# A graph layer over 200,000 edges: the window product in three bf16 parts, 29 nodes per half chunk

## The chip, the cores and the metric

One core of a Trainium2 chip runs the whole program in one launch. The metric is the time of one execution on the device, in microseconds (us), and of several executions the median counts. The core has five engines with a queue each: PE (TensorE: products and transposes into PSUM), DVE (VectorE), ACT (ScalarE), POOL (GpSimd) and SP (SyncE, which here only issues DMA transfers). Each runs its instructions in order and meets the others through semaphores.

## The reference

A graph layer on 6250 nodes with 128 features each and 200,000 edges, sorted by destination. Only what is computed by edge matters for what follows:

```python
src = jax.random.randint(..., (200000,), 0, 6250, jnp.int32)
dst = (6250 * jax.random.uniform(..., (200000,)) ** 2.0).astype(jnp.int32)
_o = jnp.argsort(dst, stable=True)
src, dst, edge_attr_4 = src[_o], dst[_o], ...
...
def mesh_conv(x, src, dst, ea, w1, b1, g, bt, w2, b2):
    m = jnp.concatenate([x[dst], x[src], ea], axis=-1) @ w1 + b1
    m = jax.nn.silu(group_norm(m, g, bt))
    m = m @ w2 + b2
    out = jax.ops.segment_sum(m, dst, num_segments=n)
    return out / jnp.clip(cnt, 1.0)[:, None]
...
h = mesh_conv(x, ...)                       # then norm, silu, + time embedding
h = mesh_conv(h, ...)                       # then norm, silu, + x
logits = (q[dst] * k[src]).sum(-1) * scale + (edge_attr @ ew + eb)
w = softmax of logits over the edges of one dst
o = jax.ops.segment_sum(w[:, :, None] * v[src], dst, num_segments=n)
return x_in + h + group_norm(o @ ow + ob, an_g, an_b)
```

All of it is fp32.

## The kernel before, in words

Edges stand in tiles of 128 (one edge a partition), eight tiles make a chunk of 1024 edges, and there are 196 chunks, the last one short (1563 tiles, `EI`). The program has three stages over all chunks: conv 1, conv 2, attention (`pipeline(i, stage)`, line 755). Ahead of them comes the preparation (lines 195 to 333), and each stage ends with `mend` and the last nodes.

*The product of a node with its edges.* The first layer's weights are applied to nodes, not edges: a table `a_d` holds each node's share as a destination, `b_d` (in attention `kv_d`) its share as a source. The source rows are gathered edge by edge, by an indirect DMA from POOL, one a tile (line 661). The destination rows are not gathered: the edges are sorted, so a chunk touches neighbouring nodes. SP loads a window of `WN` = 112 rows of `a_d` from the chunk's lowest node into `pk` (line 647), below it stand the 4 attribute weights and the bias (lines 1056 and 1260). On the other side stands `ohT`: line 631 copies each edge's offset in the window, `rel_d`, onto 112 partitions, for two chunks at a time (`LG`), and line 634 puts the 4 edge attributes and a row of ones below. ACT makes a one-hot of the offsets in two passes, a square of the difference to the partition's number (656, bias `minus_p`) and a Relu (657). One fp32 product of 117 rows a tile then gives the destination's share, the attributes' and the bias at once: `m` in the convolutions (1089), `qe` in attention (1294).

*The rest of a chunk.* In a convolution DVE adds the gathered rows (1096), ACT squares (1098), DVE reduces (1100), normalises (1111 to 1115), ACT takes the silu (1116), DVE builds a one-hot of destinations mod 128 (667), PE sums the edges into their nodes (1121, `u`), and ACT and DVE add that into the table of node sums (1126, 1131). Attention has logits (1309 to 1315), a segmented maximum for up to 8 chunks at a time (1342, 1343), weights (1365) and sums (1372). A function `in_order` (743) fixes the order of the instructions on DVE, SP, ACT and PE as the pipeline wrote them; POOL's gathers run ahead as far as buffers are free (4 in the convolutions, 11 in attention).

*Node batches and side work.* While a stage runs, finished nodes are worked off in batches of 4 windows (`conv_nodes`, 867; `attention_nodes`, 956), 10 batches a stage, at fixed places from about chunk 80 on. They store the next stage's tables. During conv 1 a side task, `deferred` (392), is taken one step a chunk from the fifth chunk on; it loads weights, prepares attention's marks, and counts what the loops below have to do. What is left of it when the first batch is due is run to its end there (lines 790 to 792).

*Edges that don't fit the window.* `relative` (305) sets the offset of every edge that lies `WN` or more beyond the chunk's lowest node to -1 and its `main` to 0; `dm0` (333) is then -1 too, so that the edge takes no part in the fast path. `deferred` finds chunks with such edges (574 to 579, 589 to 591: `trips_i`, the number of 128-node windows of such a chunk), sets `most` to the number of chunks if there is any, and from it `nout_i`, the turns of the loop at 723, and `fix_i` (426 to 440), whether `mend` runs and how many node batches it repeats. `mend` (671) is a run-time loop that is taken once or not at all; in it `leftovers` turns over the chunks, and for each chunk an inner loop (698) over its windows computes the missed edges with loads, gathers and fp32 products of its own, after which the node batches are done again one at a time. The loops of this kind have a meeting of all engines at the end of each turn.

The few lines that matter most:

```python
nc.vector.scalar_tensor_tensor(m, r, float(WN), over(good, c), ALU.is_lt, ALU.mult)        # 308
nc.vector.tensor_scalar(most, most, 0.5, float(NCH), ALU.is_gt, ALU.mult)                   # 593
nc.vector.tensor_scalar(nout_i, most, float(NCH - EI // TPC), 0.0, ALU.subtract, ALU.max)   # 594
with tc.For_i(0, some, 1):                                                                  # 676
with tc.For_i(0, n, 1) as r:                                                                # 698
with tc.For_i(0, nout, 1) as c:                                                             # 723
```

Of the kernel before, what the change touches and what calls it, by code (L numbers as in the profile page):

```python
# [38 lines left out]
KW = WN + KE  # L39
# [10 lines left out]
def kernel(ctx: ExitStack, tc: tile.TileContext, x, src, dst, eat, w, out):  # L50
# [32 lines left out]

    def by_quarter(op, n):

        q = -(-n // 4)
        for a in range(0, n, q):
            op(slice(a, min(a + q, n)))
# [14 lines left out]
    nc.vector.tensor_scalar(minus_p, iota_p, -1.0, None, ALU.mult)  # L103
# [25 lines left out]
    def attribute_rows(pool, i):  # L129
        t = pool.tile([5, D], FP, name="wcb")  # L130
        nc.sync.dma_start(out=t[0:4, :], in_=w[f"c{i}_w1"][2 * D:2 * D + 4, :])
        nc.sync.dma_start(out=t[4:5, :], in_=w[f"c{i}_b1"][None, :])
        return t

# [8 lines left out]
    a_d = {i: dram.tile([(NW + 1) * P, D], FP, name=f"a_d{i}") for i in (1, 2, 3)}  # L143
# [3 lines left out]
    web_d = dram.tile([KE, DB], FP, name="web_d")  # L147
    dwl_d = dram.tile([P, EW], FP, name="dwl_d")
    dmod_d = dram.tile([P, EW], FP, name="dmod_d")
    rel_d = dram.tile([EW, P], FP, name="rel_d")  # L150
# [7 lines left out]
    lo_i = const.tile([P, NCH], I32, name="lo_i")  # L158
# [10 lines left out]
    def by_node(table_d, wi, m):  # L169
        return table_d[wi * P:(wi + m) * P, :].rearrange("(w p) c -> p w c", p=P)  # L170

# [23 lines left out]
    with tc.tile_pool(name="node0", bufs=1) as np_, tc.tile_pool(name="prep", bufs=1) as pp, \  # L195
# [34 lines left out]
        wcb = attribute_rows(rt, 1)  # L230
        centre(rt, wcb, H)
        nc.sync.dma_start(out=wc_d[1], in_=wcb)
# [3 lines left out]
        zeros = np_.tile([P, D], FP, name="zeros")  # L236
# [6 lines left out]
        for a in range(0, NW, 4):  # L243
# [29 lines left out]
        red = pp.tile([P, 2, NCH], FP, name="red")  # L273
        redm = pp.tile([P, 2, NCH], FP, name="redm")
# [3 lines left out]
        nc.vector.tensor_reduce(red[:, 0, :], by_chunk(d_f), AX.X, ALU.min)  # L278
        nc.vector.tensor_scalar(red[:, 0, :], red[:, 0, :], -1.0, None, ALU.mult)
        nc.vector.tensor_tensor(tmp, prev_i, d_i, ALU.is_gt)  # L280
        nc.vector.tensor_scalar(by_chunk(tmp)[:, :, 0], by_chunk(tmp)[:, :, 0], not_first, None, ALU.mult)
        nc.vector.tensor_reduce(red[:, 1, :], by_chunk(tmp), AX.X, ALU.max)
        nc.gpsimd.partition_all_reduce(
            redm.rearrange("p a c -> p (a c)"), red.rearrange("p a c -> p (a c)"), P, bass_isa.ReduceOp.max)


        for a, (m, tT) in keep.items():
# [8 lines left out]
        nc.vector.tensor_scalar(low, redm[:, 0, :], -1.0, None, ALU.mult)  # L296
        good = pp.tile([P, NCH], FP, name="good")
        nc.vector.tensor_scalar(good, redm[:, 1, :], 0.5, None, ALU.is_lt)
        rel = pp.tile([P, EW], FP, name="rel")
        main = pp.tile([P, EW], FP, name="main")  # L300

        def over(t, c):
            return t[:, c, None].to_broadcast([P, c.stop - c.start, TPC])
# [8 lines left out]
        by_quarter(relative, NCH)  # L312
        for k in range(0, EW, 4 * P):
            for _ in to_rows(rel, rel_d, 1.0, pst.tile([P, 4, P], FP, name="tp"),
                             rp.tile([P, 4, P], FP, name="sb"), k, nc.scalar):
                pass

        nc.vector.tensor_copy(lo_i, low)
        nc.vector.tensor_scalar(w0_i, lo_i, 7, None, ALU.arith_shift_right)
        nc.vector.tensor_copy(w0_f, w0_i)  # L320
        lm_i = pp.tile([P, NCH], I32, name="lm_i")
        nc.vector.tensor_scalar(lm_i, lo_i, P - 1, None, ALU.bitwise_and)
        lm = pp.tile([P, NCH], FP, name="lm")
# [4 lines left out]
        dm_i = pp.tile([P, EW], I32, name="dm_i")  # L328
        nc.vector.tensor_scalar(dm_i, d_i, P - 1, None, ALU.bitwise_and)
        nc.vector.tensor_copy(tmp, dm_i)  # L330
        by_quarter(lambda a: nc.vector.scalar_tensor_tensor(
            tmp[:, a], tmp[:, a], 1.0, main[:, a], ALU.add, ALU.mult), EW)
        nc.vector.tensor_scalar(dm0, tmp, 1.0, None, ALU.subtract)


    NPK = 3
    pk = [const.tile([P, DB], FP, name=f"pk{j}") for j in range(NPK)]
# [54 lines left out]
    def deferred(dp, ps):  # L392
# [82 lines left out]
        def weights():  # L475
# [11 lines left out]
            web = dp.tile([5, DB], FP, name="web")  # L487
            nc.vector.memset(web, 0.0)
            yield
            nc.sync.dma_start(out=web[0:4, D:], in_=w["ew"])  # L490
            nc.sync.dma_start(out=web[4:5, D:], in_=w["eb"][None, :])
# [13 lines left out]
            nc.sync.dma_start(out=web_d, in_=web)  # L505

        def time():
# [15 lines left out]
            teb = dp.tile([P, KE], FP, name="teb")  # L523
            nc.vector.memset(teb, 0.0)
            nc.vector.tensor_tensor(teb[:, KE - 1:], tp[:, 0, :1], cols["tm_b"], ALU.add)
            yield
            tp = bank()
            for j in range(2):
                nc.tensor.matmul(tp[:KE, 0, :], lhsT=teb, rhs=wab[2][:, j * D:(j + 1) * D], start=(j == 0), stop=(j == 1))
            yield  # L530
            nc.vector.tensor_tensor(kept[0], kept[0], tp[:KE, 0, :], ALU.add)
            yield
            nc.sync.dma_start(out=wc_d[2], in_=kept[0])
# [333 lines left out]
    def conv_nodes(b, i, w, m, idle=0, last=False):  # L867
# [67 lines left out]
        if bias:  # L935
            yield
# [674 lines left out]
```

## Time and profile before

| what | value |
|---|---|
| median of 3 runs | 8053.96 us (8042.97 to 8057.24) |
| the profiled execution's own time; its span | 8070.85 us; 8068.5 us |
| granted PE clock, mean of the span | 0.679 of full speed |
| conv 1, conv 2, attention (first and last gather) | 55 to 2506; 2587 to 5008; 5088 to 7931 us |
| PE busy in 2560 to 5000, in 5100 to 7900 | 1231 of 2440 us; 1338 of 2800 us |
| DVE busy in the same | 1602; 1540 us |
| POOL busy in the same | 1483; 1469 us |
| DMA: gathers' queue; the other queue | 410 MB in 175,056 packets; 380 MB in 232,868 packets |
| rel_d load, pk load, attribute load | 896 KB x 291; 56 KB x 588; 40 KB x 291 |

A line of groups reads: source line, engine, operation, tile written and tiles read, shape, count, then busy time and mean ns of one, then the idle time of the engine just before them and what ended it. In the table of waits a line reads: engine, tile and line that waited, what ended the wait, then the total in us, how often, and the longest. "Remote" is a release the profile can't place, "issue" is a wait for nothing that it shows. PE's records count two passes for one fp32 product, each with a weight load of its own (PEld).

### The profile page before, as it was taken

The numbers are of one execution on the slowest core, as the hardware profiler recorded it, in microseconds if no ns is written. First come the engines' busy times: TensorE is split into PE (matmuls) and PEld (weight loads), VectorE is DVE, ScalarE is ACT, GpSimd is POOL, SyncE is SP. The second block draws the span as 40 slices with busy tenths as digits, with TensorE's granted clock in tenths as the row PEclk, the third lists the DMA queues.
The fourth block names the chain that finished last, engine by engine and source line by source line (L and its number), as shares of the span: only waits on it lengthen the run. The fifth ranks groups of instructions, "written<-read, shape, count | busy, mean of one in ns | idle before, by whom it ended". The sixth has DMA issues, their size and how long they took to land. (4 is left out here: it accounts for less than half of the span.)

```text
span 8068.5 us, 72388 instructions
## 1 busy us (share of the span) xinstructions
PE 3978.0 (49%) x20935; PEld 3656.4 (45%) x20936; DVE 4993.0 (62%) x7274; ACT 3483.6 (43%) x5592; POOL 4485.6 (56%) x4706
## 2 busy tenths in 40 slices
PE   4555545544544454555555544344444555455444
PEld 3444444444443444444544544244444444444434
DVE  5767776666654566666777766255665655565446
ACT  4555555555544455555555544122222222234444
POOL 5666666666543666666566654455555555555541
PEclk7666666777666666666777767566666666666666
DMA  5433333333322333333333332343444444444431
GB/s 136 106 91 94 92 101 85 93 87 90 89 78 60 92 87 87 92 87 93 101 96 96 96 85 72 104 121 111 116 115 117 119 119 117 115 115 128 115 106 51
DMA packets 413975, 797.97 MB, mean 99 GB/s; under 512 B 102179, under 2 KB 274966, under 8 KB 379509
## 3 DMA queue, kind: packets, MB, share of 16 engines
q0 software_dynamic: 175056, 410.03, 19.0%
q1 hardware_dynamic: 232868, 379.58, 16.5%
q10 hardware_dynamic: 5632, 3.50, 0.2%
q8 instruction: 173, 2.83, 0.2%
q14 instruction: 246, 2.02, 0.1%
HBM read 751.77 MB, written 40.96 MB: 98 GB/s over the span
## 5 line engine op out<-in xcount | busy, mean ns | idle before, releaser
L661 POOL DMA_INDIRECT g<-b_d,src_i x3126 | 2969.5, 950 | 1917.1 <-DVE h L1096 987.6
L661 POOL DMA_INDIRECT g<-kv_d,src_i x1563 | 1490.2, 953 | 1363.6 <-DVE cm L1408 537.0
L1121 PE MATMUL u<-h,oh 128*128 128x129 f32 (+1 forms) x6252 | 1330.0, 381 | 1735.7 <-ACT h L1116 867.0
L1121 PEld LDWEIGHTS u<-h,oh 128*128 128x128 f32 x6252 | 1193.7, 284 | 1860.4 <-issue 943.9
L1089 PE MATMUL m<-pk,ohT 117*128 117x128 f32 x6252 | 1066.8, 324 | 687.1 <-issue 632.2
L1089 PEld LDWEIGHTS m<-pk,ohT 117*128 117x128 f32 x6252 | 988.1, 239 | 745.1 <-issue 696.5
L1372 PE MATMUL us<-v,oh 128*128 128x145 f32 x3126 | 740.0, 399 | 905.1 <-issue 549.2
L1372 PEld LDWEIGHTS us<-v,oh 128*128 128x128 f32 x3126 | 653.5, 282 | 975.9 <-issue 949.1
L1096 DVE TENSOR_TENSOR h<-m,g 128x1024 f32<-128x1024 f32 x392 | 475.1, 1212 | 971.9 <-remote 898.2
L1294 PE MATMUL qe<-pk,ohT 117*128 117x136 f32 x3126 | 588.6, 354 | 431.0 <-issue 247.0
L1294 PEld LDWEIGHTS qe<-pk,ohT 117*128 117x128 f32 x3126 | 548.7, 258 | 473.3 <-issue 286.2
L656 ACT ACTIVATE ohT<-ohT,minus_p 112x1024 f32<-112x1024 f32 x588 | 670.5, 1140 | 42.2 <-DMA ohT<-rel_d 29.6
L1116 ACT ACTIVATE h<-h 128x1024 f32<-128x1024 f32 x392 | 412.8, 1053 | 596.7 <-DVE h L1115 299.4
L657 ACT ACTIVATE ohT<-ohT 112x1024 f32<-112x1024 f32 x588 | 619.7, 1054 | 18.6
L1126 ACT ACTIVATE u<-u,mask 128x129 f32<-128x129 f32 (+1 forms) x784 | 263.8, 336 | 823.7 <-remote 763.7
L1100 DVE TENSOR_REDUCE var<-sq 128x64 f32<-128x1024 f32 x392 | 475.3, 1212 | 192.6 <-ACT sq L1098 85.2
L667 DVE TENSOR_TENSOR oh<-cps,dm 128x1024 f32<-128x1024 f32 x392 | 474.7, 1211 | 89.4 <-remote 79.2
L1385 ACT ACTIVATE us<-d 128x16 f32<-128x16 f32 x196 | 36.7, 187 | 1042.9 <-DVE d L1382 729.6
L1114 DVE TENSOR_TENSOR h<-h,cps 128x1024 f32<-128x1024 f32 x392 | 477.2, 1217 | 14.6 <-DVE h L1111 1.3
L1115 DVE TENSOR_TENSOR h<-h,cps 128x1024 f32<-128x1024 f32 x392 | 477.1, 1217 | 13.5 <-DVE h L1114 0.2
L1098 ACT ACTIVATE sq<-h 128x1024 f32<-128x1024 f32 x392 | 411.3, 1049 | 168.7 <-DVE h L1096 136.3
L1111 DVE TENSOR_TENSOR h<-h,cps 128x1024 f32<-128x1024 f32 x392 | 474.3, 1210 | 0.0
(286 smaller groups left out, 4387.7 us busy)
## 6 DMA issues: line engine op xcount, KB each, us to landing
ohT<-rel_d SPq DMA_DIRECT2D x291, 896.0 KB
g<-b_d,src_i POOLq DMA_INDIRECT x3126
pk<-a_d SPq DMA_DIRECT2D x588, 56.0 KB
g<-kv_d,src_i POOLq DMA_INDIRECT x1563
ohT<-in_eat_dram SPq DMA_DIRECT2D x291, 40.0 KB
a_d<-n_o SPq DMA_DIRECT2D x28, 256.0 KB
kv_d<-n_o SPq DMA_DIRECT2D x28, 256.0 KB
n_h<-h_d SPq DMA_DIRECT2D x19, 256.0 KB
```

The lines of the kernel that those rows point to most:

```text
L656: nc.scalar.activation(k.ohT[:WN, :], k.ohT[:WN, :], AF.Square, bias=minus_p[:WN])
L657: nc.scalar.activation(k.ohT[:WN, :], k.ohT[:WN, :], AF.Relu, bias=1.0, scale=-4.0)
L661: nc.gpsimd.indirect_dma_start(out=g[:, t, :table_d.shape[1]], out_offset=None, in_=table_d, in_offset=bass.IndirectOffsetOnAxis(ap=k.src[ ...
L667: return nc.vector.tensor_tensor(k.oh[:, :k.nt, :], iota[:, None, :].to_broadcast([P, k.nt, P]), k.dm[:, :, None].to_broadcast([P, k.nt, P ...
L1089: nc.tensor.matmul(k.m[:, t, :], lhsT=lhs[:, t * P:(t + 1) * P], rhs=rhs, start=(j == 0), stop=(j == len(terms) - 1))
L1096: nc.vector.tensor_tensor(k.mt, k.m[:, :n], k.g[:, :n], ALU.add)
L1100: return lambda: nc.vector.tensor_reduce(var[:, at:at + n * H], sq[:, :n].rearrange("p t (g c) -> p (t g) c", c=HD), AX.X, ALU.add)
L1114: nc.vector.tensor_tensor(k.mt, k.mt, over_edges(gam, k.nt), ALU.mult)
L1115: nc.vector.tensor_tensor(k.mt, k.mt, over_edges(bet, k.nt), ALU.add)
L1121: nc.tensor.matmul(k.u[:, 0, :wide], lhsT=k.oh[:, t, :], rhs=k.h[:, t, :wide], start=(t == 0), stop=(t == k.nt - 1))
L1294: nc.tensor.matmul(k.qe[:, t // TB, at:at + DB], lhsT=lhs[:, t * P:(t + 1) * P], rhs=rhs, start=(j == 0), stop=(j == len(terms) - 1))
L1372: nc.tensor.matmul(k.u[:, :wide], lhsT=k.oh[:, t, :], rhs=k.v[:, t, :wide], start=(t == 0), stop=(t == k.nt - 1))
```

## The change

Table rows, attributes and weights are kept as a sum of three bf16 numbers (`NP` = 3: the value, the rest, the rest of the rest), each in rows of its own, so that one bf16 product over 126 rows stands for the fp32 product over 117. To have room for three rows a node, the window is 29 nodes (`WH`, three rows each: `KA` = 87), and a chunk has two windows, one for each half of its tiles; below stand three times 13 rows for attributes and bias. Offsets are compared with the partition's number divided by three. `relative` works by half chunks, and the mask holds the new width. The one-hot for the sums, the sums, the gathers and the normalisation are as before.

```diff
 KE = 5
-KW = WN + KE
+NP = 3
+WH = 29
+KA = NP * WH
+KR = NP * (KE - 1) + 1
+KW = KA + NP * KR
...
+    def parts_of(t, rest, p):
+        nc.scalar.copy(p(0), t)
+        nc.vector.tensor_tensor(rest, t, p(0), ALU.subtract)
+        nc.scalar.copy(p(1), rest)
+        nc.vector.tensor_tensor(p(2), rest, p(1), ALU.subtract)
...
-    a_d = {i: dram.tile([(NW + 1) * P, D], FP, name=f"a_d{i}") for i in (1, 2, 3)}
+    a_d = {i: dram.tile([(NW + 1) * P, NP * D], BF, name=f"a_d{i}") for i in (1, 2, 3)}
...
+    PIECE = 16 * EPC
+    ep_d = {a: dram.tile([KR, min(PIECE, EI * P - a)], BF, name=f"ep_d{a}") for a in range(0, EI * P, PIECE)}
...
-    rel_d = dram.tile([EW, P], FP, name="rel_d")
+    rel_d = dram.tile([EW, P], BF, name="rel_d")
...
+    def attributes(n, cast, engine, pool, queue):
+        a = n * PIECE
+        to = ep_d[a]
...
+        for k in range(4):
+            queue.dma_start(out=t[k * SEG:(k + 1) * SEG, :],
+                            in_=eat[k, a:a + length].rearrange("(s l) -> s l", l=span))
+        yield
+        for j in range(NP - 1):
+            cast(p[j], t)
+            yield
+            engine.tensor_tensor(t if j < NP - 2 else p[NP - 1], t, p[j], ALU.subtract)
+            yield
+        for j in range(NP):
+            queue.dma_start(
+                out=to[4 * j:4 * j + 4, :].rearrange("k l -> (k l)").rearrange("(s l) -> s l", l=span), in_=p[j])
+        queue.dma_start(out=to[KR - 1, :].rearrange("(p l) -> p l", p=P), in_=ones[:, :length // P])
+        yield
...
+        def table_a(a):
+            m, tT = keep[a]
             o = pso.tile([P, 4, P], FP, name="o")
             for i in range(m):
                 nc.tensor.matmul(o[:, i, :], lhsT=tT[:, i, :], rhs=wab[1][:, :D], start=True, stop=True)
-            b = rt.tile([P, 4, D], FP, name="a0")
-            nc.scalar.copy(b[:, :m, :], o[:, :m, :])
-            last = nc.sync.dma_start(out=by_node(a_d[1], a, m), in_=b[:, :m, :])
+            b = rp.tile([P, 4, NP, D], BF, name="a0")
+            r = rp.tile([P, 4, D], FP, name="a0r")
+            parts_of(o[:, :m, :], r[:, :m, :], lambda j: b[:, :m, j, :])
+            nc.sync.dma_start(out=by_node(a_d[1], a, m), in_=b[:, :m, :, :].rearrange("p w j c -> p w (j c)"))
...
         def relative(c):
-            r, m = by_chunk(rel)[:, c, :], by_chunk(main)[:, c, :]
-            nc.vector.tensor_tensor(r, by_chunk(d_f)[:, c, :], over(low, c), ALU.subtract)
-            nc.vector.scalar_tensor_tensor(m, r, float(WN), over(good, c), ALU.is_lt, ALU.mult)
+            r, m = by_half(rel)[:, c, :], by_half(main)[:, c, :]
+            nc.vector.tensor_tensor(r, by_half(d_f)[:, c, :], over(halves, c), ALU.subtract)
+            nc.vector.scalar_tensor_tensor(m, r, float(WH), over(good, c), ALU.is_lt, ALU.mult)
...
+        for a in keep:
+            if a not in soon:
+                table_a(a)
...
     (deferred)
+        for n in range(2, len(ep_d)):
+            yield from attributes(n, nc.scalar.copy, nc.vector, ep, nc.sync)
         yield from batches()
...
     (load_group)
         nc.sync.dma_start(
-            out=f[:WN, :m * P],
-            in_=rel_d[c * TPC:c * TPC + m, :].rearrange("t p -> (t p)")[None, :].to_broadcast([WN, m * P]))
-        nc.sync.dma_start(out=f[WN:KW, :m * P], in_=eat[:, c * EPC:c * EPC + m * P])
+            out=f[:KA, :m * P],
+            in_=rel_d[c * TPC:c * TPC + m, :].rearrange("t p -> (t p)")[None, :].to_broadcast([KA, m * P]))
+        for j in range(NP):
+            nc.sync.dma_start(out=f[KA + j * KR:KA + (j + 1) * KR, :m * P], in_=ep_d[...][:, ...])
...
     (loads)
-        nc.sync.dma_start(out=k.pk[:WN, :D], in_=rows_d[bass.ds(first, WN), :])
+        for h in range(halves):
+            nc.sync.dma_start(out=k.pk[:KA, h, :D], in_=rows_d[bass.ds(first[h], KA), :])
...
     (conv_nodes, the table of destinations)
+        nc.scalar.copy(p[:, :, 0, :], t)
+        yield
+        nc.vector.tensor_tensor(t, t, p[:, :, 0, :], ALU.subtract)
+        yield
+        nc.scalar.copy(p[:, :, 1, :], t)
+        yield
+        nc.vector.tensor_tensor(p[:, :, 2, :], t, p[:, :, 1, :], ALU.subtract)
+        yield
-        nc.sync.dma_start(out=rows_of(done[0], w, m), in_=done[1])
+        nc.sync.dma_start(out=rows_of(done[0], w, m), in_=p.rearrange("p w j c -> p w (j c)"))
...
-                    hidden(k, [(k.ohT[:KW], k.pk[:KW, :D])])
+                    hidden(k, [(k.ohT[:KW], lambda t: k.pk[:KW, 2 * t // TPC, :D])])
```

In the loops of `mend` the window's rows are loaded as three parts and added up to fp32 (two additions a pass); the loops themselves, `most`, `nout_i` and `fix_i` are as before.

More of the change, by code (lines that the diff above doesn't have):

```diff
@@ L170, in by_node @@
         return table_d[wi * P:(wi + m) * P, :].rearrange("(w p) c -> p w c", p=P)
+    SEG = 32
+    def attributes(n, cast, engine, pool, queue):
+        a = n * PIECE
+        to = ep_d[a]
+        length = to.shape[1]
+        span = length // SEG
+        t = pool.tile([4 * SEG, PIECE // SEG], FP, name="e_t")[:, :span]
+        p = [pool.tile([4 * SEG, PIECE // SEG], BF, name=f"e_p{j}")[:, :span] for j in range(NP)]
+        for k in range(4):
[12 more added lines that the diff above has]
+        yield
     def to_rows(t, d_, scale, ps, sb, k, queue):
@@ L229 @@
         centre(rt, wab[1], 2 * H)
-        wcb = attribute_rows(rt, 1)
+        wcb = attribute_rows(pp, 1)
         centre(rt, wcb, H)
-        nc.sync.dma_start(out=wc_d[1], in_=wcb)
+        store_constants(pp, wcb, wc_d[1], wp_d[1], D)
         load_row(nc.scalar, "c1_g")
         load_row(nc.scalar, "c1_bt")
-        zeros = np_.tile([P, D], FP, name="zeros")
+        nc.gpsimd.memset(ones, 1.0)
+        for n in range(2):
+            for _ in attributes(n, nc.gpsimd.tensor_copy, nc.gpsimd, rp, nc.scalar):
+                pass
+        zeros = np_.tile([P, NP * D], BF, name="zeros")
         nc.vector.memset(zeros, 0.0)
@@ L299 @@
-        rel = pp.tile([P, EW], FP, name="rel")
+            b = rp.tile([P, 4, NP, D], BF, name="a0")
+            r = rp.tile([P, 4, D], FP, name="a0r")
+            parts_of(o[:, :m, :], r[:, :m, :], lambda j: b[:, :m, j, :])
+            nc.sync.dma_start(out=by_node(a_d[1], a, m), in_=b[:, :m, :, :].rearrange("p w j c -> p w (j c)"))
+        soon = list(keep)[:2]
+        for a in soon:
+            table_a(a)
+        halves = pp.tile([P, 2 * NCH], FP, name="halves")
+        nc.vector.tensor_scalar(halves, redm, 0.0, -1.0, ALU.min, ALU.mult)
@@ L333 @@
         nc.vector.tensor_scalar(dm0, tmp, 1.0, None, ALU.subtract)
+        for a in keep:
+            if a not in soon:
+                table_a(a)
     NPK = 3
-    pk = [const.tile([P, DB], FP, name=f"pk{j}") for j in range(NPK)]
+    pk = [const.tile([P, 2, DB], BF, name=f"pk{j}") for j in range(NPK)]
     for t in pk:
@@ L732, in left_rows @@
         nc.vector.memset(k.rows[:, D:], 0.0)
-        nc.sync.dma_start(out=k.rows[:, :D], in_=rows_d[bass.ds(k.win * P, P), :])
+        parts = lp.tile([P, NP, D], BF, name="l_parts")
+        nc.sync.dma_start(out=parts.rearrange("p j c -> p (j c)"), in_=rows_d[bass.ds(k.win * P, P), :])
+        nc.vector.tensor_tensor(k.rows[:, :D], parts[:, 0, :], parts[:, 1, :], ALU.add)
+        nc.vector.tensor_tensor(k.rows[:, :D], k.rows[:, :D], parts[:, 2, :], ALU.add)
         onehot(k, pools, iota_j)
@@ L1079, in conv @@
             if i == 1:
-                aside = deferred(side.enter_context(tc.tile_pool(name="dp", bufs=1)), nd)
+                aside = deferred(side.enter_context(tc.tile_pool(name="dp", bufs=1)), nd,
+                                 side.enter_context(tc.tile_pool(name="ep", bufs=2)))
             def over_edges(r, n):
@@ L1437, in products @@
             def products(self, k):
-                products(k, [(k.ohT[:KW], k.pk[:KW])])
+                products(k, [(k.ohT[:KW], lambda t: k.pk[:KW, 2 * t // TPC])])
             def first(self, k):
@@ L1538, in left @@
             gather(k, k.g, kv_d)
-            products(k, [(k.ohf.rearrange("p t e -> p (t e)"), k.rows), (k.ea, webl)])
+            products(k, [(k.ohf.rearrange("p t e -> p (t e)"), lambda t: k.rows), (k.ea, lambda t: webl)])
             lg = lp.tile([P, TPC, H], FP, name="l_lg")
```

128 lines of the change are left out of this document (82 added, 46 removed).

## The prediction

> **What bounds the kernel now.** I read the page first (busy shares and costly groups), then the table of waits, then the order of time inside one stretch of the first half, and last the instructions of the loops that close a stage (line 676). No engine is near full: PE 49%, DVE 62%, POOL 56% of 8068.5 us.
>
> ```profile
> span 8068.5 us, 72388 instructions
> ...
> PE 3978.0 (49%) x20935; PEld 3656.4 (45%) x20936; DVE 4993.0 (62%) x7274; ACT 3483.6 (43%) x5592; POOL 4485.6 (56%) x4706
> ...
> L661 POOL DMA_INDIRECT g<-b_d,src_i x3126 | 2969.5, 950 | 1917.1 <-DVE h L1096 987.6
> ...
> L1089 PE MATMUL m<-pk,ohT 117*128 117x128 f32 x6252 | 1066.8, 324 | 687.1 <-issue 632.2
> ```
>
> The first row to keep is POOL's: a gather is busy 0.95 us and starts 1.25 us after the last one, so eight of them make 10.0 us a chunk, the least a chunk can cost. A chunk of a convolution takes 12.4 us (conv 2: first add at 2604, last at 5039, 196 chunks). The rest is in the waits:
>
> ```profile
> POOL g L661 <- DVE h L1096: 987.6, 172, 21.6
> ...
> DVE h L1096 <- remote: 898.2, 139, 32.8
> ...
> PE u L1121 <- issue: 860.4, 517, 14.4
> ```
>
> POOL waits for buffers that the add at 1096 frees, the add waits for products that PE delivers late, and PE waits for nothing that the profile shows. The order of time shows how:
>
> ```profile
> 2001.85 1.49 PE L1121 MATMUL u<-h,oh 128*128 128x129 f32 x7 [3.16 <-issue]
> ...
> 2004.45 0.37 PE L1121 MATMUL u<-h,oh 128*128 128x129 f32 x1 [1.12 <-issue]
> ...
> 2007.28 0.37 PE L1121 MATMUL u<-h,oh 128*128 128x129 f32 x1 [2.45 <-issue]
> ...
> 2015.53 0.94 POOL L661 DMA_INDIRECT g<-b_d,src_i  x1 [0.30 <-issue]
> ...
> 2020.74 3.63 PE L1089 MATMUL m<-pk,ohT 117*128 117x128 f32 x16
> ...
> 2027.51 0.95 POOL L661 DMA_INDIRECT g<-b_d,src_i  x1 [11.04 <-DVE h L1096]
> ```
>
> Seven passes go in 1.5 us, then single ones 1.4 to 2.8 us apart, until about 3 us after POOL's unbroken row of gathers has ended; then sixteen in 3.6 us. In the trace's records this happens in 217 episodes, 2151 us in all: a row of gathers begins, PE gets through about 64 matmul passes (quartiles 63 and 69), and from there it crawls until the row ends. A chunk has 32 passes (16 for m or qe, 16 for u or us).
>
> **The part that decides: the windows.** The reference draws a destination as 6250 times the square of a uniform number, 200,000 of them, sorted. Near node n there are 200000/(2*sqrt(6250*n)) edges a node: 16 at the top. A half chunk has 512 edges, so at the top it spans 512/16 = 32 nodes; the new half window holds 29 (the old one held 112 for a chunk of 64). Counting the drawn destinations: 39 of 391 halves span more than 29 nodes (up to 35), in 25 chunks from number 163 on; no chunk spans more than 66. The edges beyond the window are masked out of the fast path and sent to the loops of `mend`, which the old kernel skips. One missed edge anywhere sets `most`, and with it: 195 turns of the outer loop of `leftovers` in each of the three stages, whether a chunk has missed edges or not; inside them 36 passes a stage (a chunk times its 128-node windows, counted the same way); and all 10 node batches again. The trace shows what it costs to skip all this:
>
> ```profile
> L676 PEldq EVENT_SEMAPHORE  x42: 51/51/442, 2562.8 to 8047.1; - x42
> ...
> L676 PEldq COMPARE_BRANCH  x9: 70/183/3703, 2562.1 to 8047.3; - x9
> ```
>
> One skip is 14 semaphore waits and 3 branches on PE, and takes from 5052.93 to 5060.03, 7.1 us, of which one branch is 3.34 us (a jump over code; 3.70 in another skip).
>
> **Each step, with its price.**
> - *Outer turns*, 3 x 195 = 585. A turn is such a skip of the inner loop plus a register load (0.31 us, line 675) and the barrier of its way back. I take 7 us, the measured skip: 4095 us. Bounds: 3.8 us without the slow branch (2223 us), 10.4 us with two (6084 us).
> - *Passes of a convolution*, 2 x 36 = 72, nothing overlapped with a neighbour because every engine meets at the end of a turn. Sources loaded 3 us (a register load 0.47, an issue 0.35, landing about 2); eight gathers 10.0; the last one's landing 2; then one after the other add 1.22 (1096), square 1.05, reduction 1.21, root 0.43, reciprocal 0.5, three passes of `normed` 3.66, silu 1.05, sixteen passes of u 3.6, add 0.42: 28 us, and 5 for entry and barrier: 33 us, 2376 us. One-hot, transposes and fp32 products lie under the gathers.
> - *Passes of attention*, 36. The same 15 us to the landed rows; logits 2.7; then 16 times, through one PSUM buffer, four transposes (1.06 us for four at line 823), a 512-column DVE pass (0.68) and two handovers (0.2): 31; `me`, exp, weighting, sums, merge 12; loop 5: 66 us, 2376 us. Bounds for both kinds of pass: a fifth less (3800 together), two fifths more (6650).
> - *Batches again*, 3 x 10, each alone: about 24 us, the chain of lines 880 to 937 with its stores; 720 us (500 to 1000).
> - *PE's passes*: m and qe fall from 16 to 8 a chunk (one bf16 pass for two fp32 ones), so a chunk has 24 and a row of gathers reaches 64 after 2.7 chunks instead of 2.0. POOL's waits for DVE (988 in the convolutions, 537 + 313 in attention: 1838 us) come once a row; a quarter fewer is 460, and I take 420 since node batches add passes that don't change. Bounds: 0 and 1838. PE's own faster product counts nothing beside it.
> - *The side work* (`deferred`) gets 66 more steps ahead of what it did, 6 for each of 11 attribute pieces, and is run to its end before the first batch, at chunk 81 or so. It ended there by itself before; now 63 DVE instructions come in one go, 36 us of DVE work, with two rounds of loads, eight groups of transposes and their stores in a chain, some 85 us, while POOL fills four buffers. Chunk 82 and all behind it on DVE wait. Counting what is caught up: +65 (20 to 100).
> - *Start*: `table_a` adds two ACT copies' and two subtractions' work to 13 groups, 11 of them now behind `relative`; first window loads wait for the last store: +18 (0 to 35).
> - *Node batches*: two copies (0.59) and two subtractions (0.68) for each of 28, spread, and twice in the tails: +32 (0 to 75).
> - *Loads*: rel_d falls from 896 to 348 KB; pk goes as two loads of 256-byte rows; attributes as three of 13 rows; SP issues 8 a pair of chunks for 4, at 0.35 us each, and waits most of its time anyway. The line that meets them is the compare (656), which waited 29.6 us in all for rel_d. I take 0; bounds -30, and +160: 40 of 291 loads are used less than 10 us after issue, 4 us late each.
> - DVE, ACT and POOL work of the main loops is the same in number and columns.
>
> [...]
>
> [...]
>
> **Sum.** Main part 8070.85 - 420 + 65 + 18 + 32 = 7766. Loops 4095 + 2376 + 2376 + 720 = 9567. Together 17,333, against a profiled execution of 8070.85 (span 8068.5); the runs' median is 8053.96, 17 less, so 17,316.
>
> **Rivals.**
> - *The loops are cheap* (chance 0.20): branches hit, handovers overlap. For it: seven of the nine PE branches took 0.07 to 0.32 us, and the first skip, which had no slow one, 3.0 us. 7766 + 2223 + 3800 + 500 = 14,290.
> - *The loops are dear* (0.14): every turn fetches code twice, passes too. For it: two of the three skips had a slow branch on PE. 7766 + 6084 + 6650 + 1000 = 21,500.
> - *The other side: faster* (0.03). The loops are not entered, because the mask I read as excluding offsets 29 and up doesn't flag these edges, and PE's crawl decides: 8070 - 420 + 115 = 7766. Against it: the comparison with `WH` and the count of 39 halves. It decides only if no edge at all is missed, since one sets all turns.
> - *No loops, but late loads* (0.02): 7766 + 420 + 160, about 8350: the crawl is not relieved and the compare waits.
>
> **How the numbers follow.** Forecast 0.61, at 17,316, its own range 14,900 to 20,500. With half of each neighbour the range is 14,000 to 21,500, leaving out under 2 in 10. Faster by over 0.2% (about what a measurement of this kernel can tell from no change): 0.03, the third rival; same 0.01; slower 0.96.
>
> **What would show it.** Right: three stretches at the stages' ends, thousands of us each, with PE, DVE and ACT nearly idle, POOL in groups of 8 gathers far apart, 288 + 288 + 288 more gathers (4689 to 5553), the inner loop's branches entered 585 times and taken 108, a bare turn near 7 us, passes near 33 and 66; in the convolutions rows of gathers longer than 16 and 24. Wrong: `mend` skipped; or stages that end at once; or a turn under 3 us.

## The result, and the profile after

The changed kernel takes 15,997.68 us (median of 4 runs, 15,968.67 to 16,013.41) where the kernel before takes 8,055.6 us (4 runs, 8,042.97 to 8,058.16): 1.986 times as long, 95% interval 1.983 to 1.990. The profiled execution took 16,013.41 us, its span is 16,011.7 us, and PE's granted clock was 0.561 of full speed, for 0.679 before.

First the page of the changed kernel: the span, the busy shares, and two groups that the kernel before doesn't have.

```profile
span 16011.7 us, 196079 instructions
...
PE 5943.1 (37%) x26014; PEld 4911.0 (31%) x26015; DVE 6788.4 (42%) x11548; ACT 4292.7 (27%) x6769; POOL 5329.3 (33%) x5579
...
L760 POOL DMA_INDIRECT g<-b_d,l_src x576 | 555.0, 964 | 3568.9 <-DMA l_dw<-dwl_d 3113.7
...
L796 DVE COPY kf<-w_f 128x1 f32 x588 | 90.5, 154 | 2328.2 <-PEq L822 2315.4
```

Every engine's share fell, and there are 124,000 more instructions. `l_src` is a tile of the loops of `mend`: 576 gathers of a convolution's rows are 72 passes of eight. Line 796 is the first statement of a turn of the loop over chunks; DVE waits 2315 us there for PE's end of the turn before. So the loops run. How often, the instructions of the inner loop (797) and of the outer one (822) say; a row has the count, then shortest, median and longest in ns, then the first and the last start:

```profile
L797 PEldq EVENT_SEMAPHORE  x7668: 51/51/4222, 2670.5 to 15827.9; - x197
...
L797 PEldq COMPARE_BRANCH  x1797: 64/181/342, 2670.4 to 15828.0; - x200
...
L797 DVEq MOVE  x108: 36/36/43, 3375.3 to 15756.4; - x108
...
L822 DVEq MOVE  x585: 36/43/49, 2672.2 to 15755.2; - x195
```

585 turns, three times 195, and 108 passes taken. And no branch on PE in them took longer than 0.342 us: the branch of 3.34 us that the kernel before showed when it skipped the loops once is not among the 1797.

The busy time of each engine in six windows shows what the loops take: for each stage first the turns and passes, then the node batches done again (columns: window, its length, then busy us and instructions of PE, PE's weight loads, DVE, ACT and POOL, then PE's granted clock, the DMA engines' share and GB/s).

```profile
2668.40:4705.90 2037.50, 622.00 (x2022) 465.88 (x2020) 375.95 (x739) 224.89 (x257) 279.47 (x288) 0.52 0.04 12
4705.90:4952.60 246.70, 84.64 (x320) 67.80 (x320) 55.46 (x143) 73.60 (x101) 0.00 (x0) 0.50 0.09 27
7452.00:9478.00 2026.00, 619.96 (x2016) 464.82 (x2016) 369.12 (x736) 223.12 (x252) 275.57 (x288) 0.51 0.04 12
9478.00:9777.00 299.00, 105.36 (x400) 85.58 (x400) 92.56 (x170) 66.19 (x91) 0.00 (x0) 0.50 0.13 40
12658.00:15828.80 3170.80, 1411.25 (x4896) 1008.99 (x4896) 764.94 (x2248) 132.54 (x324) 276.15 (x288) 0.51 0.05 13
15828.80:15995.00 166.20, 31.91 (x120) 24.96 (x120) 64.32 (x112) 41.69 (x51) 0.00 (x0) 0.50 0.16 48
sum 7946.20, PE 2875.11 PEld 2118.04 DVE 1722.35 ACT 762.03 POOL 831.19; mean PE 479.19 PEld 353.01 DVE 287.06 ACT 127.00 POOL 138.53
```

The loops take 7946 us. The rest is 16,011.7 - 7946.2 = 8065.5 us, and the rest of the kernel before, without its three skips (3.0 + 7.1 + 6.3 us), is 8052.1. So the loops are the whole of the loss, and all the rest of the change together, the faster product included, moved the other 8052 us by +13 us.

The 7946 us divide as follows. From the start of one turn to the next, a turn that does nothing takes 4.27 us (median of 510 in three stages; shortest 4.19). Of the turns with passes, 42 have one and 33 two in the three stages; a convolution's take 36.7 and 71.2 us, attention's 68.3 and 134.1.

| term | measured | predicted |
|---|---|---|
| outer turns, 585 | 585 x 4.27 = 2498 | 4095 |
| passes in the convolutions, 72 | 2037.5 + 2026.0 - 390 x 4.27 = 2398; 33.3 each | 2376 |
| passes in attention, 36 | 3170.8 - 195 x 4.27 = 2338; 64.9 each | 2376 |
| node batches again, 30 | 246.7 + 299.0 + 166.2 = 712; 23.7 each | 720 |
| the main part | 8067 (with 2 around the span) | 7766 |

Where the main part's +13 us come from, stage by stage, each from the end of the skip or loops before to its own: conv 1 +106, conv 2 +11, attention -100, the end after the last loop -4. In conv 1 two places hold all of it. The first gather starts 14 us later than before and the 33rd 42; from there to the 680th the distance is 25 to 42. Then the side work is run out in front of the first node batch. The order of time at that place, POOL alone (start, us, engine, line, operation; in brackets how long the engine was idle before, and who ended it):

```profile
1105.74 0.94 POOL L760 DMA_INDIRECT g<-b_d,src_i  x1 [0.30 <-issue]
...
1179.56 0.94 POOL L760 DMA_INDIRECT g<-b_d,src_i  x1 [72.87 <-DVE h L1209]
```

POOL stops for 72.9 us, and the distance is 92 to 112 us from there to the end of the stage (101 at its last gather): what is lost there isn't caught up.

In the second convolution, the same stretch of both kernels, the table of waits. Before:

```profile
DVE h L1096 <- remote: 494.0, 71, 32.8
POOL g L661 <- DVE h L1096: 475.2, 84, 17.5
```

After:

```profile
POOL g L760 <- DVE h L1209: 476.4, 79, 17.5
...
DVE h L1209 <- remote: 391.5, 69, 16.7
```

The product has half the passes, and POOL's wait for the add is the same to 1.2 us.

### The profile page after: what moved, and what is told of

It reads as the page before. It is cut to its first block, busy times and chain, and to the rows that moved or that the text cites. A ratio compares the mean times of both kernels' runs of the same rounds, so it can differ in the third digit from the quotient of the medians.

```text
span 16011.7 us, 196079 instructions
## 1 busy us (share of the span) xinstructions
PE 5943.1 (37%) x26014; PEld 4911.0 (31%) x26015; DVE 6788.4 (42%) x11548; ACT 4292.7 (27%) x6769; POOL 5329.3 (33%) x5579
## 5 line engine op out<-in xcount | busy, mean ns | idle before, releaser
L1234 PE MATMUL u<-h,oh 128*128 128x129 f32 (+1 forms) x7404 | 1753.9, 421 | 3241.6 <-ACT h L1229 1993.9
L1234 PEld LDWEIGHTS u<-h,oh 128*128 128x128 f32 x7404 | 1589.2, 321 | 3393.2 <-ACT h L1229 2068.6
L760 POOL DMA_INDIRECT g<-b_d,l_src x576 | 555.0, 964 | 3568.9 <-DMA l_dw<-dwl_d 3113.7
L1485 PE MATMUL us<-v,oh 128*128 128x145 f32 (+1 forms) x3702 | 901.4, 431 | 905.6 <-DVE nm L1518 394.0
L1663 PE MATMUL blk<-ident,l_lg 128*128 128x128 f32 x2304 | 640.8, 434 | 538.0 <-DVE l_part L1664 427.9
L755 ACT ACTIVATE ohT<-ohT,minus_p 87x1024 bf16<-87x1024 bf16 x588 | 668.7, 1137 | 76.1 <-DMA ohT<-rel_d 38.5
L1664 DVE CUSTOM_DVE_ANT_0 l_junk<-blk,l_neg 128x512 f32<-128x512 f32 x576 | 398.7, 692 | 681.0 <-PE blk L1663 681.0
L1663 PEld LDWEIGHTS blk<-ident,l_lg 128*128 128x128 f32 x2304 | 411.3, 217 | 764.5 <-DVE l_part L1664 644.0
L1422 DVE TENSOR_TENSOR g<-qe,g 128x768 f32<-128x768 f32 (+1 forms) x463 | 298.5, 686 | 804.5 <-PE qe L1407 448.7
L756 ACT ACTIVATE ohT<-ohT 87x1024 bf16<-87x1024 bf16 x588 | 619.6, 1054 | 18.6
```

What stands on the lines that cost most here:

```text
L755: nc.scalar.activation(k.ohT[:KA, :], k.ohT[:KA, :], AF.Square, bias=minus_p[:KA])
L756: nc.scalar.activation(k.ohT[:KA, :], k.ohT[:KA, :], AF.Relu, bias=1.0, scale=-4.0)
L760: nc.gpsimd.indirect_dma_start(out=g[:, t, :table_d.shape[1]], out_offset=None, in_=table_d, in_offset=bass.IndirectOffsetOnAxis(ap=k.src[ ...
L1234: nc.tensor.matmul(k.u[:, 0, :wide], lhsT=k.oh[:, t, :], rhs=k.h[:, t, :wide], start=(t == 0), stop=(t == k.nt - 1))
L1422: nc.vector.tensor_tensor(kk, qe[:, :, :, :D], kk, ALU.mult)
L1485: nc.tensor.matmul(k.u[:, :wide], lhsT=k.oh[:, t, :], rhs=k.v[:, t, :wide], start=(t == 0), stop=(t == k.nt - 1))
```

## The experiments

Ratios are to the kernel before, run beside each on the same chip. Where two changed kernels are compared in us, the two runs can be from two chips, on which the kernel before differed by up to 14 us (8046 to 8060).

**no_mend**: the main part alone.

```diff
-        nc.vector.tensor_scalar(most, most, 0.5, float(NCH), ALU.is_gt, ALU.mult)
+        nc.vector.tensor_scalar(most, most, 0.5, 0.0, ALU.is_gt, ALU.mult)
```

> The changed kernel with the count that sends it into the loops set to zero, so the 1388 edges that lie beyond a 29-node window stay out of the sums; the main part is left as it is. Theory A (read from the trace of the changed kernel: the loops take 2284 + 2325 + 3337 = 7946 us and the main part of the work did not get faster): 16,012 - 7,946 + 16 for skipping the loops = about 8,080 us, within 1% of the kernel before. Theory B (the prediction's main part: PE's crawl relieved by 420 us): 7,766 us, a ratio of 0.964.

Measured: 8076.67 us (10 runs), ratio 1.0012 (0.9992 to 1.0033). Theory A. Without the loops the change brings nothing that can be measured, and the loops are all of the doubling.

**turns_from_160**: the price of a turn that does nothing.

```diff
-        with tc.For_i(0, nout, 1) as c:
+        with tc.For_i(160, nout, 1) as c:
```

> The outer loop over chunks starts at chunk 160 instead of 0; no chunk below 163 has a missed edge, so 480 turns of the three stages that do nothing are left out and nothing else. Theory A (a turn that does nothing costs 4.27 us, as the trace shows): 480 x 4.27 = 2050 us less, 13,950 us. Theory B (the prediction's 7 us a turn): 3360 us less, 12,640 us. Theory C (the turns cost nothing of their own, the passes and batches make the time): no change, 16,000 us.

Measured: 13,969 us in one run, 2029 us less than the changed kernel's median: 4.23 us a turn. Theory A; 7 us a turn and turns for nothing are both out. The turns that are left can be counted in its profile:

```profile
L822 DVEq MOVE  x105: 36/36/49, 2655.5 to 13710.9; - x105
```

**before_window_64**: the same loss without any of the change.

```diff
-            nc.vector.scalar_tensor_tensor(m, r, float(WN), over(good, c), ALU.is_lt, ALU.mult)
+            nc.vector.scalar_tensor_tensor(m, r, float(64), over(good, c), ALU.is_lt, ALU.mult)
```

> The kernel before, fp32 product and all, with only the number in its window test changed from 112 to 64 nodes: 101 edges in 5 of 196 chunks then miss it. Nothing of the bf16 change is in it. Theory A (missing any edge is what costs; turns at 4.27 us, a convolution's pass 33, attention's 65, the node batches once more 708): 8,055 + 585 x 4.27 + 16 x 33 + 8 x 65 + 708 = about 12,310 us. Theory B (the prediction's 7 us a turn): 13,900 us. Theory C (the loops cost only where edges are missed): 8,055 + 1,048 + 708 = 9,810 us.

Measured: 12,270 us in one run. Theory A, to 40 us. The fp32 kernel pays 4200 us for 101 edges of 200,000, with all 585 turns and 24 passes (lines 723 and 698 of the kernel before):

```profile
L723 DVEq MOVE  x585: 36/43/43, 2556.5 to 12013.2; - x195
...
L698 DVEq MOVE  x24: 36/36/55, 3331.6 to 12014.4; - x24
```

**quarter_windows**: a window for every 256 edges, so that none is missed.

```diff
 WH = 29
+WP = 4
...
-        return t.rearrange("p (c t) -> p c t", t=TPC // 2)
+        return t.rearrange("p (c t) -> p c t", t=TPC // WP)
...
-    pk = [const.tile([P, 2, DB], BF, name=f"pk{j}") for j in range(NPK)]
+    pk = [const.tile([P, WP, DB], BF, name=f"pk{j}") for j in range(NPK)]
...
-        halves = 1 + (k.nt > TPC // 2)
+        halves = -(-k.nt * WP // TPC)
...
-                    hidden(k, [(k.ohT[:KW], lambda t: k.pk[:KW, 2 * t // TPC, :D])])
+                    hidden(k, [(k.ohT[:KW], lambda t: k.pk[:KW, WP * t // TPC, :D])])
```

> The changed kernel with four windows of 29 nodes a chunk, one for 256 edges, in place of two: by the drawn destinations no quarter spans more than 18 nodes, so no edge is missed and the loops are skipped without leaving anything out. Two more window loads a chunk go out on SP's queue. Theory A (main part unchanged by the bf16 product): as the run without loops, 8,080 us, plus 0 to 100 for the loads. Theory B (the main part is 7,766 and SP has room): 7,766 us.

Measured: 8132.25 us (4 runs), ratio 1.0096 (1.0073 to 1.0118). Theory A. It takes back 7865 us of the loss and is still not faster than the kernel before.

**side_work_spread**: quarter windows, and the side work in time.

```diff
             if n > 4:
                 next(aside, None)
+                next(aside, None)
```

> The quarter-window kernel with two steps of the side work a chunk instead of one, so that it comes to its own end before the first node batch instead of being run out in one go at chunk 82. Theory A (POOL's stop of 73 us at chunk 82 is lost time): quarter_windows' 8,132 less some 70, about 8,060 us, level with the kernel before. Theory B (the convolution catches up behind the stop, as the prediction half assumed): no more than 20 us less, 8,110 us or more.

Measured: 8077.31 us (10 runs), ratio 1.0022 (1.0002 to 1.0041): 55 us less than quarter_windows, which ran on another chip; by the two ratios it is 60. Between the theories, nearer A. By POOL's gathers the stop at chunk 82 is gone, but the distance to the kernel before, 38 us at the 64th gather, had grown to 57 by the 680th: spread out, the extra steps cost DVE some 20 us of their own.

**passes_as_before**: the number of passes alone.

```diff
-                        nc.tensor.matmul(k.m[:, t, :], lhsT=lhs[:, t * P:(t + 1) * P], rhs=rhs(t),
+                        for a in (slice(0, D // 2), slice(D // 2, D)) if len(terms) == 1 else (slice(0, D),):
+                            nc.tensor.matmul(k.m[:, t, a], lhsT=lhs[:, t * P:(t + 1) * P], rhs=rhs(t)[:, a],
...
     (the same in attention's products, for qe)
```

> As side_work_spread, with every bf16 product of 128 (136) columns issued as two of 64 (68), so that PE issues 32 passes a chunk as the kernel before does, for 24; nothing else is changed. Theory A (PE's results reach the other engines late because of how long POOL's row of gathers has lasted; the number of passes hardly matters): the convolutions stay as they are within 30 us each; attention gives back some of its 100 us; 0 to +130 us on side_work_spread. Theory B (the prediction: 64 passes into a row PE crawls, so a third more passes means a third more waits): +420 us or more, 8,480 us.

Measured: 8180.45 us (4 runs), ratio 1.0164 (1.0147 to 1.0181): 103 us on side_work_spread. Theory A. From the first gather of a stage to its last, in one profile of each, conv 1 changes by -12, conv 2 by +27, attention by +68 us (two profiles of side_work_spread differ by up to 17 us a stage). So eight passes fewer a chunk are worth about 100 us, most of it in attention, not 420.

**three_row_buffers** and **five_row_buffers**: how long POOL's rows of gathers get.

```diff
-    gp_conv = gpc.enter_context(tc.tile_pool(name="gpc", bufs=4))
+    gp_conv = gpc.enter_context(tc.tile_pool(name="gpc", bufs=3))
...
     (the other kernel has bufs=5, and bufs=1 for the tile a0r and the pool ep)
```

> As side_work_spread, with three buffers for gathered rows in the convolutions instead of four, so that POOL's rows of gathers end after 16 where they now reach 24; 16 gathers see 48 of PE's passes. Theory A (PE's results are held from some 9 us into a row until it ends, and the wait comes once a row whatever its length): more rows, each with its 4 to 5 us; (20 + 5) / 2 = 12.5 us a chunk for 11.9 and 390 chunks, +200 to +300 us. Theory B (64 passes into a row PE crawls; shorter rows never get there): the waits go, -200 us or more in the two convolutions.

> As side_work_spread, with five buffers for gathered rows in the convolutions instead of four (paid for by single instead of double staging in two places of the set-up and side work), so that rows of gathers can reach 32. Theory A (one wait of about 5 us a row whatever its length): (40 + 5) / 4 = 11.3 us a chunk for 11.9, about -150 us in the two convolutions and under 7,950 us, faster than the kernel before. Theory B (64 passes, then a crawl): a fourth chunk in the row is all crawl; no change or slower.

Measured: 8085.3 us (one run) with three, 8078.94 us (10 runs, ratio 1.0034, 1.0021 to 1.0047) with five: 8 and 2 us on the 8077 with four. With three buffers both theories missed. With five the time is what Theory B allowed, no change, but its crawl had also called for 200 us less with three. So neither the prediction's crawl after 64 passes nor one fixed wait for each row of gathers can be the rule. What POOL loses in the second convolution hardly moves in any of these kernels. Counted are the starts of gathers more than 1.6 us apart, and what they have beyond the usual 1.25:

| kernel | such waits | us lost, conv 2 | us lost, attention |
|---|---|---|---|
| before | 89 | 463 | 884 |
| no_mend | 90 | 473 | 796 |
| quarter_windows | 109 | 452 | 844 |
| side_work_spread | 108 | 446 | 835 |
| passes_as_before | 107 | 477 | 907 |
| three_row_buffers | 107 | 460 | 820 |
| five_row_buffers | 115 | 447 | 847 |

In the second convolution that is some 0.3 us for each of 1563 gathers, whatever the number of passes, of buffers and of waits; in attention it is 0.5 to 0.6, most with the most passes.

**no_gather_busy_pool**: POOL as busy as with gathers, but no gathers.

```diff
...
+        for t in range(10):
+            at = t % (table_d.shape[1] // D) * D
+            nc.gpsimd.memset(g[:, :k.nt, at:at + D], 0.25)
-        for t in range(k.nt):
-            nc.gpsimd.indirect_dma_start(
...
```

> As side_work_spread, but in the main part each chunk's eight gathers are replaced by ten fills of the gathered tile by POOL (1024 columns each, some 0.9 to 1.0 us by the fills of the profile), so POOL is as busy for a chunk and waits for the same buffers, while no row is gathered; the source nodes' share is left out of the sums. Theory A (PE's results come late because of the gathers, and the 0.3 us lost for each gather in a convolution and 0.5 in attention hang on that): these waits go; about 10.3 us a chunk in every stage, 587 x 10.3 + 340 outside = 6,400 us. Theory B (the engines' own chain of a chunk takes 11.9 to 14 us, POOL only waits for it): no change, 8,000 us or more.

**rows_by_plain_loads**: the same bytes without POOL.

```diff
...
+        for t in range(k.nt):
+            nc.sync.dma_start(out=g[:, t, :table_d.shape[1]], in_=table_d[a + t * P:a + (t + 1) * P, :])
-        for t in range(k.nt):
-            nc.gpsimd.indirect_dma_start(
...
```

> As side_work_spread, but in the main part each chunk's eight gathers are replaced by eight plain loads on SP's queue of 128 consecutive rows, the same bytes into the same tiles; POOL has no work in a chunk, and wrong rows enter the sums. Theory A1 (it is the transfers that hold PE's results back): no gain over the gathers' waits, 11.5 us a chunk or more, 7,500 us or more. Theory A2 (it is POOL's issuing of gathers that does): DVE with 8.3 us a chunk becomes the limit; some 9.5 us a chunk, 587 x 9.5 + 340 = 5,900 us. Theory B (the engines' own chain): 8,000 us.

Measured: 6085.48 and 6218.47 us, one run each; but the kernel before, unchanged, took 6220.29 us beside them on that chip, in its one run. On a chip where, by the estimate of 6232 us at the end, next to nothing is lost to waits, the two say nothing about where it is lost. The first, and side_work_spread, were run again.

> The same kernel as side_work_spread once more, because the last two runs fell on a chip on which the kernel before took 6,220 us and not 8,055, and a comparison needs both kernels on one chip. Where the kernel before takes 8,055: again 8,077 (ratio 1.002). Where it takes 6,220: Theory A (there PE's results are not late, POOL's gathers at 10.0 us a chunk set the pace, and PE's faster product is off that path): 6,220 plus the start's 36 and some of the side work, 6,230 to 6,290 us, ratio 1.00 to 1.01. Theory B (the prediction's: fewer passes are worth their 100 us or more anywhere): 6,120 us or less.

> The same kernel as no_gather_busy_pool once more, beside the kernel before on one chip; the source nodes' share is left out of the sums. Where the kernel before takes 8,055: Theory A (the gathers make PE's results late) 6,100 to 6,400 us; Theory B (the engines' own chain) 8,000 us or more. Where it takes 6,220, the two theories do not part: about 6,085 us again.

Measured, on a chip where the kernel before took 8045.92 us (13 runs): side_work_spread again 8073.97 us, ratio 1.0027 (1.0008 to 1.0046); without gathers 6087.5 us in one run. Theory A, though 12 us under its range. Of the 1986 us between the two, some 100 are POOL's own: from its first fill to its last, a chunk's ten fills take 10.0 us in both convolutions, as eight gathers 1.25 apart do, and 9.5 in attention. The rest goes with the gathers. So does what sets the two chips apart: the kernel without gathers takes 6085 us on the one and 6088 on the other (one run each), the kernel before 6220 (one run) and 8046. How the add of a convolution then waits, in the groups of that kernel (the add is its line 1217, the product 1210, POOL's fills 769):

```profile
L769 POOL MEMSET g<- 128x1024 f32 x5880 | 5437.1, 949 | 409.9 <-DVE v L1486 65.1 <-DVE h L1217 64.2 <-SPq L782 50.0
...
L1217 DVE TENSOR_TENSOR h<-m,g 128x1024 f32<-128x1024 f32 x392 | 477.2, 1217 | 342.3 <-POOL g L769 321.4 <-DMA ohT<-ep_d 14.0 <-PE m L1210 5.5
```

The add waits for POOL, as it should where POOL sets the pace, and 5.5 us in all for PE.

## Why the prediction was right, and where it was not

**The windows: right.** 25 chunks, 36 passes a stage and all 195 turns came out to the count: 585 turns, 108 passes, 864 more gathers. (The 39 halves beyond 29 nodes are a count of the input; no trace shows them.) That a few missed edges set all turns is shown by before_window_64, with 101. The forecast of 17,316 us was 1318 us, 8%, too high. It is the difference of two larger errors, 1597 us too much for the turns and 301 too little for the main part; that they had opposite signs was luck.

**The outer turns: the term that was mis-sized, 4095 us for 2498.** The step took the skip of a loop in the kernel before, 7.1 us with a branch of 3.34 us in it, for a turn. In the loop this branch doesn't come: 1797 branches, none above 0.342 us. What is left is PE's chain of 13 semaphore waits, four branches, a register load (0.30 us) and the meeting, together 4.27 us, close to the bound of 3.8 that the prediction named. turns_from_160 shows the price by taking turns away.

Attention's turns, at 4.28 us (median), are no dearer than the convolutions' 4.27, though the body that they skip is longer: 136 PE instructions a pass (4896 in 36) for 28 (2022 in 72), by the windows. What the branch of 3.34 us waited for, no run shows.

**Passes and batches: right.** 33.3 us for 33, 64.9 for 66, 23.7 for 24. That fits a chain with little beside it; the windows show PE busy 31% of the first loop and POOL 14%.

**PE's crawl: the step that failed, -420 us for about -100.** The prediction had the add wait for products that PE delivers late: PE gets through 64 passes of a row of gathers and then crawls, so that fewer passes make longer rows and a quarter fewer waits. The crawl itself did shrink. Counted from the first gap of 0.8 to 6 us inside a group of passes to the end of POOL's row, it fell from 551 to 257 us in conv 2 and from 627 to 76 in attention; it begins after a median of 68 passes in conv 2 before and 56 after, so 64 is no fixed number. But POOL's waits did not follow in the convolutions (463 to 466 us), and in attention by 109 only. The order of time of the changed kernel shows why. In attention, start and length of the instructions in turn:

```profile
10614.11 4.20 PE L1485 MATMUL us<-v,oh 128*128 128x145 f32 x16 [5.06 <-DVE v L1478]
...
10623.32 3.88 PE L1485 MATMUL us<-v,oh 128*128 128x145 f32 x16 [4.10 <-issue]
...
10633.01 0.95 POOL L760 DMA_INDIRECT g<-kv_d,src_i  x1 [0.30 <-issue]
10637.95 0.16 DVE L1518 SCALAR_TENSOR_TENSOR nm<-us,nm 128x2 f32<-128x2 f32 x1 [15.28 <-remote]
```

PE issues the sums of two chunks without a break, by 10,618.3 and 10,627.2. Line 1518 needs the first of the two and nothing else (the program merges a chunk's sums after it has issued the next chunk's). DVE is idle from 10,622.7, and is released at 10,637.95, 4 us after the last gather of POOL's row and 19.6 us after the passes that it needs. In the second convolution:

```profile
5321.63 1.00 PE L1202 MATMUL m<-pk,ohT 126*128 126x128 bf16 x8
...
5326.55 3.78 PE L1234 MATMUL u<-h,oh 128*128 128x128 f32 x16 [3.92 <-ACT h L1229]
...
5330.12 1.06 PE L1202 MATMUL m<-pk,ohT 126*128 126x128 bf16 x8
...
5344.78 1.23 DVE L1209 TENSOR_TENSOR h<-m,g 128x1024 f32<-128x1024 f32 x1 [7.64 <-remote]
5344.78 0.72 ACT L1239 ACTIVATE u<-u,mask 128x128 f32<-128x128 f32 x2 [7.62 <-remote]
```

PE issues a chunk's product one chunk ahead, so the add at 5344.78 uses the product of 5321.63, through at 5322.6; the one at 5330.12 is the next add's. The last thing that this add needs is another: it writes one of four buffers `h`, and the sums of the chunk four before, which read that buffer, are the 16 passes from 5326.55, through at 5330.33. The add starts 14.5 us after them, in the same 10 ns as ACT's copy of these very sums. So what is late is not the passes but the news of them, and it is news of the sums, whose 16 fp32 passes the change left as they were. The trace's records of PE's semaphore say the same: the update that belongs to the pass that ended at 5330.33 stands at 5344.76, and in attention those of four passes that ended from 10,618.3 to 10,627.2 stand between 10,637.9 and 10,638.2.

Counted over conv 2: an add is late if it starts over 0.5 us after DVE is free and its product and those sums have ended. Before, that was so for 78 of 196 adds, 519 us; after, for 80 of 196, 449 us. For all but 3 of either kernel's late adds the sums were the last thing needed, and all but 3 of the 158 start within 0.1 us after an update of PE's semaphore. Where the passes needed had ended within 9 us of a row's first gather, 4 of 80 adds were late before and 6 of 63 after; where they ended later in a row, 74 of 94 and 74 of 117. ACT's copies of the sums lost 413 us before and 336 after, the sums used by line 1518 in attention (1405 in the kernel before) 549 and 418. Why PE's passes crawl at all, no run shows.

That the lateness comes with POOL's gathers is shown by no_gather_busy_pool_2: counted in the same way, none of its 196 adds and none of its 196 copies in conv 2 is late. Whether it is their issue or their transfers, and why it should hold back PE's news, stays open; rows_by_plain_loads would have told it apart, but fell on the other chip.

**Side work: right.** +65 predicted, 73 us of standstill, none caught up; the 20 us that it costs even when spread were not in the estimate.

**Start: 36 for 18, just over its upper bound of 35.** 14 us until the first gather, the rest until the 33rd.

**Node batches and loads: within their bounds.** What conv 1 has besides start and side work is within 10 us, conv 2 has +11. The rel_d load lands later although it carries 348 KB for 896: in the DMA records the last packet of it and of the attribute loads issued right behind it ended 7.4 us (median) after its issue, for 4.6 before. It costs next to nothing: the compare waited 38.5 us for it in all, for 29.6 before. The 4 us late each, from which the prediction has its bound of +160 us and its rival with late loads, no run shows: the last packet came 2.8 us later, and the compare's waits grew by 8.9 us in all.

```profile
  DMA ohT<-rel_d: 38.5, 13
```

**The rivals.** The cheap loops had the turns nearest (2223 for 2498) and passes and batches too low; the dear ones, with two slow branches in every turn, are out: none of the 1797 took longer than 0.342 us, and that a turn fetches code was assumed; no run shows it. Loops not entered is out by the 585 turns; what the main part would then take, 7766 us, is out by no_mend, and so are late loads.

No kernel of the study that computes every edge beats the kernel before. The nearest, side_work_spread, is 0.2 to 0.3% slower: 100 us won by fewer passes, given to the start, the side work and two more window loads a chunk.

## What to carry to other kernels

When a tile gets narrower, count the data against the new limit before costing the instructions: 1388 of 200,000 edges fell out here, and the fallback charged mostly by the loop, 2498 us in turns and 712 in batches that no missed edge needed. Price a loop's turn from the turn's own chain and not from a single skip: the three skips here took 3.0, 7.1 and 6.3 us, a turn 4.27. And before a faster engine is credited with the waits behind it, look whether the waits end when its work ends: here they ended 14 and 20 us after it in the two stretches shown, and halving the passes of the product moved 100 us of 8077. Look also at which of its results the wait is for: a buffer that must come free can be the last thing needed, and not the input.

## What the runs showed of the hardware that was not expected

- PE's results reach DVE and ACT late while POOL issues a long row of gathers: where the passes needed ended more than 9 us into the row, 74 of 94 adds of conv 2 before and 74 of 117 after; earlier in a row 4 of 80 and 6 of 63; with POOL equally busy on fills, none of 196.
- The kernel before took 6220 us in one run on one chip, where three other chips gave 8046 to 8060 us (medians of 13 to 19 runs). 588 chunks at POOL's 10.0 us and the 352 us that the kernel before spends outside its three stretches of gathers (8068.5 - 2453.3 - 2420.6 - 2842.8) make 6232 as an estimate, by which POOL waited for next to nothing there. No profile of that run is kept.
- Records of semaphore updates are missing where there are gathers: the kernel before has 1383 for 1525 due of PE and 3729 for 5801 of DVE, side_work_spread 2092 for 2394 and 3368 for 5917, no_gather_busy_pool_2 has all of them. Whether PE's late results have to do with that was not tried.
